# An attention and feed-forward kernel: the order of the work behind the last scores, and three smaller moves of order

## The chip, the cores and the metric

The kernel runs on one core of a Trainium2 chip. The core has five engines that run side by side and meet only through semaphores: TensorE (PE) multiplies matrices, VectorE (DVE) and ScalarE (ACT) work on rows, GpSimd (POOL) does a part of the element-wise work, and SyncE (SP) issues most of the transfers. Each engine executes its own queue in order. Data lies in SBUF (128 partitions); TensorE writes into PSUM, which has eight banks of 512 floats per partition.

The metric is device time in microseconds (us) of one execution, as the median of several. The reader will also meet the span: the time from the first to the last instruction in one profiled execution.

## The reference

A hidden state of 1024 rows by 512 columns goes through attention and then through a feed-forward stage with a router. Both are followed by a layer norm and added to their input:

```
x = x + layernorm(attention(layernorm(x), w_q, w_k, w_v, w_o))
x = x + layernorm(ffn(layernorm(x), base_W, base_b, router_W, router_b, A, B, expert_map))

attention: 32 query heads of 128 columns, 8 key/value heads, causal, softmax(q k / sqrt(128)) v, then w_o
ffn:       base   = x base_W + base_b
           probs  = softmax(x router_W + router_b)        15 columns
           top 8 of probs, mapped to 8 experts -> weight w of each expert
           lora   = (x A * w) B * 2                       8 experts of rank 16
           result = base + lora
```

Everything is in 32-bit floats.

## The kernel before, in words

The 1024 rows are eight row tiles of 128 rows. Attention is cut into 64 blocks: one block is one key/value group g (of eight) and one row tile t. Two neighbouring row tiles of a group are a pair (g, u). The groups 0 to 5 run one after the other; the groups 6 and 7 are interleaved pair by pair, in the order u = 0, 3, 2, 1. So the last blocks are (6,2), (6,3), (7,2), (7,3). The last four row tiles that are completed are named c, d, e, f: tiles 4, 5, 2, 3.

**One block.** `scores` (L601) runs four times per block, once for each 32 rows of the four query heads. It multiplies q and k (tile `s`, in one of two PSUM buffers), adds the mask, takes the negated row maximum `nmax`, computes the exponential with its row sum `total` (tile `p`). Two steps are left to be done inside the next call: `rescale` (L629: the reciprocal `rec` and the multiplication of `p` by it) and `finish` (L634: the transpose of `p` into `T`; after the block's fourth scores, `to_keys` starts 16 transfers that turn `T` into `K`). Two blocks later `weighted_values` multiplies `K` and v (tile `po`, one bank) and copies the result to `attnT`.

**One pair.** Two more blocks on, `project_o_pair` (L711) multiplies a pair's `attnT` with w_o by a scheme with seven half-size products instead of eight. It needs four sums and differences on VectorE first (L720 to L723: `sums` and `attnT`). Its products are `pa` to `pe`; each is merged into `acc`, the running output of the row tiles, by VectorE (L742 for group 0, L744 else). The pieces of the list are, in order, pa (4 pieces), pb (2), pc (2), pd (2), pe (4) and a last step (L751). The last group uses the plain `project_o` (`pO`, merged on L686).

**A completed row tile** then runs through `ffn_norms` (layer norm, adding x, second layer norm to `h`), `ffn_router` (transposes `ptx_h` to `hT`, router products `pl`, exponential, and `route`, eight small VectorE steps from `recr` to `hw`), and `ffn_out` (L840: base products and the transpose `ptw` of `hw`, then `finish` with the last product in `pf`; then y, its statistics, its norm, and the addition to `acc`, L870), and is stored. In `layernorm` (L282) VectorE makes statistics, aggregate and `ve`, GpSimd takes the power -1/2 of one column (`rstd`, L294), and the norm follows on VectorE (L300) or, with a `shift`, on ScalarE (L304).

**PSUM.** Tag `pm` has three banks, which all products other than scores and `po` share. Tag `s` has two buffers, for scores; the base products of some row tiles use these too.

**What sets the order.** A planner orders each engine's instructions by program order and readiness in its own model. An instruction wrapped in `keep` or `order` stays in program order among all instructions so wrapped on its engine; matmuls and transfers always are. The merges, the four sums and many copies are not wrapped in the loop over blocks. In that loop (L1019 to L1074) each block has a list of pieces `then`, of which `run_share` (L962) issues one quarter by cost behind each of the four scores. Small VectorE work waits in the list `deferred`; `work_off` (L587) takes some of it in each `scores`. Behind the loop (L1077 to L1110) the order is written out by hand: `held` takes the place of `deferred`, with one list of steps for each of the rows c, d, e, f, and `go(d, f)` executes the next step of row d and then of row f.

**At the beginning** `input_norms` (L325) normalises the eight input rows: for each row statistics, aggregate, `ve`, the power on GpSimd (`begin`), and then the norm of the row before (`end`).

Of the kernel before, what the change touches and what calls it, by code (L numbers as in the profile page):

```python
# [9 lines left out]
F32 = mybir.dt.float32  # L10
I32 = mybir.dt.int32
AF = mybir.ActivationFunctionType
ALU = mybir.AluOpType
AX = mybir.AxisListType

P = 128
# [6 lines left out]
def kernel(  # L23
# [301 lines left out]
    def input_norms(rows):  # L325

        mvs, rstds = {}, {}

        def begin(t):
            stats = small.tile([P, 6], F32, tag="stats", name=f"stats_x{t}")  # L330
            keep(nc.vector.bn_stats(stats, x_in[:, t, :]))
            mv = mvs[t] = small.tile([P, 2], F32, tag="mv", name=f"mv_x{t}")
            keep(nc.vector.bn_aggr(mv, stats))
            ve = small.tile([P, 1], F32, tag="ve", name=f"ve_x{t}")
            keep(nc.vector.tensor_scalar(ve, mv[:, 1:2], EPS, None, ALU.add))
            rstds[t] = small.tile([P, 1], F32, tag="rstd", name=f"rstd_x{t}")
            keep(nc.gpsimd.tensor_tensor(rstds[t], ve, neg_half, ALU.pow))

        def end(t):
            row = x_in[:, t, :]  # L340
            keep(nc.vector.tensor_scalar(row, row, mvs[t][:, 0:1], rstds[t], ALU.subtract, ALU.mult))

        for n, t in enumerate(rows):
            begin(t)
            if n:
                end(rows[n - 1])
        end(rows[-1])

    def input_turn(t):
# [251 lines left out]
    def scores(g, t, j):  # L601

        n = t * P + (j + 1) * SQ
        full = (t + 1) * P
        name = f"{g}_{t}_{j}"
        s = ps_s.tile([P, S], F32, tag="s", name=f"s_{name}")
        for c0 in range(0, n, QB):
            w = min(QB, n - c0)
            matmul(
                s[:, c0 : c0 + w],  # L610
                qTs[g, t // 2][:, (t % 2) * NSUB + j, :, :].rearrange("p h q -> p (h q)"),
                kTs[g, c0 // QB][:, :w],
                start=True,
                stop=True,
            )
        pin = keep if blocks.index((g, t)) >= N2 + 2 else lambda ins: ins
        rescale_scores()
        keep(nc.vector.tensor_tensor(s[:, n - SQ : n], s[:, n - SQ : n], smask, ALU.add))  # L618
        nmax = small.tile([P, 1], F32, tag="nmax", name=f"nmax_{name}")
        keep(nc.vector.tensor_reduce(nmax, s[:, :n], AX.X, ALU.max, negate=True))  # L620
        p = act.tile([P, S], F32, tag="p", name=f"p_{name}", bufs=3)
        if n < full:
            nc.gpsimd.memset(p[:, n:full], 0.0)  # L623
        total = small.tile([P, 1], F32, tag="total", name=f"total_{name}")
        keep(nc.scalar.activation(p[:, :n], s[:, :n], AF.Exp, bias=nmax, accum_out=total))  # L625
        finish_scores()
        work_off(1 + len(deferred) // 5)

        def rescale():  # L629
            rec = small.tile([P, 1], F32, tag="rec", name=f"rec_{name}")  # L630
            keep(nc.vector.reciprocal(rec, total))  # L631
            keep(nc.scalar.mul(p[:, :n], p[:, :n], rec))  # L632

        def finish():  # L634
            if j == 0:
                turned[g, t] = turn_view(turn_tile("T", g, t), t)
            pin(
                nc.vector.transpose(  # L638
                    turned[g, t][:, :, j, :, :].rearrange("p b k q -> p k b q"),
                    p[:, :full].rearrange("p (k b q) -> p k b q", b=R, q=SQ),  # L640
                )
            )
            if j == NSUB - 1:
                three = (nc.sync, nc.sync, nc.gpsimd)

                at = blocks.index((g, t))
                short = at < 1 or at < N2 and g % 2 and t in (1, 2, 3)
                alone = not short and at < N - 1
                to_keys(g, t, by=three[:1] if alone else three)

        score_tile["rescale"], score_tile["finish"] = rescale, finish
# [59 lines left out]
    def project_o_pair(g, u):  # L711
# [4 lines left out]
        a2 = attnT.pop((g, 2 * u + 1)).rearrange("p (h q) -> p h q", q=P)  # L716
        a11, a12, a21, a22 = a1[:, :hk], a1[:, hk:], a2[:, :hk], a2[:, hk:]
        sums = act.tile([P, 3, hk, P], F32, tag="sums", name=f"sums_{g}_{u}", bufs=1)
        s1, s2, s4 = (sums[:, n] for n in range(3))
        nc.vector.tensor_tensor(s1, a21, a22, ALU.add)  # L720
        nc.vector.tensor_tensor(s2, s1, a11, ALU.subtract)
        nc.vector.tensor_tensor(a21, a11, a21, ALU.subtract)
        nc.vector.tensor_tensor(s4, a12, s2, ALU.subtract)  # L723
        b11, t12, b21, b22 = wo[:, :hk, :hn], wo[:, :hk, hn:], wo[:, hk:, :hn], wo[:, hk:, hn:]
        to = sums_o[u]
        pm = {}
# [113 lines left out]
    def ffn_out(t):  # L840

        pf = []

        def base(k):
            if k == 0:

                if t in (c, e, f):
                    pf.append(ps_s.tile([P, S], F32, tag="s", name=f"pf_{t}")[:, :512])
                else:
                    pf.append(bank(f"pf_{t}"))  # L850
            matmul(pf[0], state["hT", t][:, k, :], weights["base", k], start=(k == 0), stop=False)

        def turn_hw():
            pt = bank(f"ptw_{t}")
            transpose(pt[:, :ER], state.pop(("hw", t)).rearrange("p e r -> p (e r)"), ident)
            hwT = state["hwT", t] = ffn.tile([ER, P], F32, tag="hwT", name=f"hwT_{t}")
            copy = nc.scalar.copy(hwT, pt[:, :P])
            if held:
                keep(copy)

        def finish():
            matmul(pf[0], state.pop(("hwT", t)), bt_sb, start=False, stop=True)
            y = ffn.tile([P, H], F32, tag="hy", name=f"y_{t}", bufs=3)
            order(nc.vector.tensor_tensor(y, pf[0], bias_bc, ALU.add))
            by = nc.vector if t == f else nc.gpsimd
            statistics, norm = layernorm(y, y, f"y{t}", nc.vector if t == f else nc.scalar)

            def add_y():
                norm()
                order(by.tensor_tensor(acc[t], y, acc[t], ALU.add))  # L870
                state["done", t] = True

            defer(t, statistics, add_y)

        w = [(512, lambda k=k: base(k)) for k in range(KC)]
        return w[:2], [(P, turn_hw)], w[2:], [(512, finish)]

    def ffn_store(t):
        assert state["done", t]
# [79 lines left out]
        for _, f in pieces:  # L959
            f()  # L960

    def run_share(pieces, n, m):  # L962

        total = sum(c for c, _ in pieces)
        at = 0
        for c, f in pieces:
            mid = at + c / 2
            if n * total / m <= mid < (n + 1) * total / m:
                f()
            at += c  # L970

# [47 lines left out]
    for i in range(N):  # L1019
# [4 lines left out]
        for t in complete(i, 3):  # L1024
            o = project_o(*blocks[i - 3])
        if i % 2 == 0 and i >= 4 and blocks[i - 4][0] < G - 1:
            o_pair = project_o_pair(*pairs[i // 2 - 2])
        for t in complete(i, 6, 7):
            ends = sum(ffn_out(t), [])
# [9 lines left out]
        if i % 2 and i // 2 + 1 in QW and blocks[i][1] > 1 and i > 3:  # L1039
            cut = len(rest) * 3 // 5  # L1040
            q, rest = weave(q, rest[:cut]), rest[cut:]
        then = begins[:1] + q + ends[:-1] + rest[:4] + ends[-1:] + rest[4:]
        for n in range(NSUB):
            scores(*blocks[i], n)
            run_share(then, n, NSUB)
            m = i // 2 + 1
            if i % 2 == 0 and m in QW:
                if n == 0 and i < N2:
                    combine_x(pairs[m][1], m)
                if n == (1 if i < N2 else 0):  # L1050
                    combine_q(m)
            g, t = blocks[i]
            if g % 2 and g + 1 < G and n == 1:
                if t == 6:
                    combine_k(g + 1)
                if t == 7:
                    combine_v((g + 1) // GV)
            if (i, n) in ((N2, 3), (N2 + 1, 2), (N2 + 2, 2)):
                combine_x(i - N2 + 1, 0)
# [25 lines left out]
        ffn_store(t)  # L1085
    (turn_d, products_d), (turn_e, products_e), (turn_f, products_f) = map(ffn_router, (d, e, f))
    out_c, out_d, out_e, out_f = map(ffn_out, (c, d, e, f))
    run(o_pair[:8] + out_c[0] + out_c[2] + o_pair[8:16] + [turn_d] + o_pair[16:])
    run(attend(N - 2) + [products_d])
    go(d)  # L1090
    run(out_c[1] + project_o(*blocks[N - 2]))
    go(e)
    run(out_c[3])
    go(e, e)
    run(attend(N - 1) + project_o(*blocks[N - 1]))
    go(e, f, c, f, f)
    run(out_d[0] + out_d[1] + out_d[2] + [turn_e] + out_d[3])
    go(f, c)
    run([products_e])
    go(d, e)  # L1100
    run(out_e[0] + out_e[2][:1] + [turn_f] + out_e[2][1:] + [products_f])
    go(d, f)
    run(out_f[0] + out_e[1] + out_f[2][:1] + out_e[3])
    go(e)
    run(out_f[2][1:] + out_f[1])
    go(e)
    run(out_f[3])
    go(f, f)
    for t in (c, d, e, f):
        ffn_store(t)  # L1110

# [40 lines left out]
```

## Time and profile before

| | |
|---|---|
| device time, median of 3 runs | 1064.53 us (1063.63 to 1064.58) |
| device time of the profiled execution | 1063.05 us |
| span of the profiled execution | 1061.3 us |
| mean granted TensorE clock | 0.997 |
| VectorE busy / ScalarE busy | 748.8 us / 478.2 us |
| TensorE busy between 66 and 1000 us | 932.26 of 934.00 us |
| TensorE busy between 1000 and 1052 us | 49.19 of 52.00 us |
| TensorE busy behind 1052 us | 0.15 of 9.30 us |

The span is shorter than the device time by what lies before the first and behind the last instruction. A group in the profile is named by its engine, the line of the program, what it writes and what it reads: "DVE L744 acc<-pa" is VectorE's merge of the product pa. Most matmuls are recorded on L103, which is inside a helper, so the tile's name tells which product it is. A wait is the idle time of an engine ahead of an instruction, with the event that ended it. All times count from the start of the span.

### The profile page before, as it was taken

The page shows a single profiled execution, that of the slowest core. Times are in us where ns is not written, and L with a number is a line of the kernel's source. Part 1 is how long each engine was busy: PE and PEld are TensorE (multiplying, and loading weights), DVE is VectorE, ACT ScalarE, POOL GpSimd, SP SyncE. Part 2 cuts the span into 40 slices and gives each one's busy share as a digit, 9 for nine tenths or more (in the row PEclk, how much of TensorE's full clock was granted, in tenths as well). Part 3 has the DMA queues.
Part 4 walks back from the last instruction along what each step waited for, and adds up shares of the span by engine and source line. Part 5 has one row for each costly group of instructions (what it writes and reads, how often), then busy time and mean ns, then how long its engine had stood idle before and what let it go on. Part 6 is the DMA issues. An engine that isn't in the chain of part 4 may idle for free.

```text
span 1061.3 us, 15618 instructions
## 1 busy us (share of the span) xinstructions
PE 1044.3 (98%) x4854; PEld 730.7 (69%) x4854; DVE 748.8 (71%) x1828; ACT 478.2 (45%) x962; POOL 269.4 (25%) x503
## 2 busy tenths in 40 slices
PE   9999999999999999999999999999999999999996
PEld 7766677767777676767777667767888467466543
DVE  4586657876687766877477776886667966566756
ACT  2655435553344544554244544654334654353421
POOL 2613125241131214241130313442152110111212
PEclk9999999999999999999999999999999999999998
DMA  5146352563125442453324352464333764534331
GB/s 188 33 107 159 72 121 70 152 153 89 24 54 157 102 111 70 117 154 75 70 50 129 100 124 58 131 166 110 87 108 95 169 159 110 146 92 105 80 84 40
DMA packets 78513, 111.99 MB, mean 106 GB/s; under 512 B 18176, under 2 KB 49920, under 8 KB 78432
## 3 DMA queue, kind: packets, MB, share of 16 engines
q1 hardware_dynamic: 74960, 105.71, 39.7%
q0 software_dynamic: 2096, 3.46, 1.4%
q10 hardware_dynamic: 1376, 1.84, 0.5%
q8 instruction: 39, 0.64, 0.3%
q14 instruction: 42, 0.34, 0.1%
HBM read 33.34 MB, written 2.10 MB: 33 GB/s over the span
## 4 chain that ended last, share of the span: by engine, by line
PE 93%; DVE 3%; SPq 1%; ACT 1%; DMA 1%; issue 1%; POOL 0%; POOLq 0%; DVEq 0%; ACTq 0%
PE po L103 23%; PE s L103 21%; PE pq L103 19%; PE pv L103 5%; PE pk L103 5%; PE pe L103 4%; PE pa L103 4%; PE pf L103 3%; PE pO L103 3%; PE pc L103 2%; PE pb L103 2%; PE pd L103 2%; SPq L109 1%; PE pl L103 1%; DVE T L638 1%
## 5 line engine op out<-in xcount | busy, mean ns | idle before, releaser
L632 ACT ACTIVATE p<-p,rec 128x32 f32<-128x32 f32 (+31 forms) x256 | 188.1, 735 | 240.8 <-DVE rec L631 182.2
L103 PE MATMUL po<-K,v 128*128 128x512 f32 x576 | 280.5, 594 | 0.4 <-DMA wo<-in_w_o_dram 0.3
L103 PE MATMUL s<-kT,qT 128*128 128x512 f32 (+15 forms) x768 | 272.4, 464 | 1.3 <-ACT p L625 1.3
L625 ACT ACTIVATE p<-s,nmax 128x32 f32<-128x32 f32 (+31 forms) x256 | 179.3, 700 | 161.3 <-DVE nmax L620 144.8
L638 DVE STREAM_TRANSPOSE T<-p 128x128 f32<-128x128 f32 (+7 forms) x256 | 197.7, 774 | 54.3 <-ACT p L632 42.1
L103 PEld LDWEIGHTS s<-kT,qT 128*128 128x128 f32 x768 | 140.6, 190 | 117.7 <-issue 105.9
L620 DVE TENSOR_REDUCE nmax<-s 128x1 f32<-128x32 f32 (+31 forms) x256 | 180.2, 704 | 7.3
L103 PEld LDWEIGHTS po<-K,v 128*128 128x128 f32 x576 | 103.5, 190 | 59.9 <-issue 50.2
L623 POOL MEMSET p<- 128x96 f32 (+2 forms) x192 | 29.2, 156 | 421.1 <-DVE T L638 387.8
L618 DVE TENSOR_TENSOR s<-s,smask 128x32 f32<-128x32 f32 x256 | 48.0, 187 | 87.8 <-PE s L103 86.9
L103 PE MATMUL pq<-xnT,wq 128*128 128x128 f32 (+1 forms) x608 | 97.5, 308 | 0.0
L103 PEld LDWEIGHTS pq<-xnT,wq 128*128 128x128 f32 x608 | 87.5, 191 | 11.3 <-issue 6.6
L450 DVE TENSOR_TENSOR qT<-pq,qT 128x256 f32<-128x256 f32 x156 | 69.9, 461 | 35.8 <-ACT qT L476 19.8
L188 POOL TENSOR_TENSOR tx<-xnT 128x256 f32<-128x256 f32 x52 | 37.8, 727 | 184.3 <-PE pv L103 95.2
L669 ACT COPY attnT<-po 128x512 f32<-128x512 f32 x64 | 37.3, 583 | 73.1 <-PE po L103 72.8
L103 PE MATMUL pa<-wo,attnT 128*128 128x256 f32 x224 | 58.5, 385 | 0.0
L103 PEld LDWEIGHTS pq<-tx,wq 128*128 128x128 f32 x416 | 53.0, 192 | 7.9 <-issue 7.5
L103 PE MATMUL pq<-tx,sq 128*128 128x128 f32 x416 | 57.5, 275 | 0.0
L103 PEld LDWEIGHTS pq<-tx,sq 128*128 128x128 f32 x416 | 53.4, 192 | 5.7 <-issue 5.0
L103 PE MATMUL pq<-tx,wq 128*128 128x128 f32 x416 | 55.4, 275 | 0.0
L103 PEld LDWEIGHTS pa<-wo,attnT 128*128 128x128 f32 x224 | 41.1, 190 | 14.1 <-issue 9.3
L625 ACT ACTIVATION_READ_ACCUMULATOR p<-s,nmax 128x1 f32 x256 | 49.6, 194 | 0.0
(146 smaller groups left out, 1277.0 us busy)
## 6 DMA issues: line engine op xcount, KB each, us to landing
K<-T SPq DMA_DIRECT2D x128, 128.0 KB, 2.4
K<-T SPq DMA_DIRECT2D x128, 112.0 KB, 2.3
wq<-in_w_q_dram SPq DMA_DIRECT2D x27, 512.0 KB, 5.0
K<-T SPq DMA_DIRECT2D x128, 96.0 KB, 2.2
K<-T SPq DMA_DIRECT2D x128, 80.0 KB, 2.1
wo<-in_w_o_dram SPq DMA_DIRECT2D x32, 256.0 KB, 3.8
K<-T SPq DMA_DIRECT2D x108, 64.0 KB, 2.0
K<-T SPq DMA_DIRECT2D x113, 48.0 KB, 2.0
```

The costliest lines, as they stand in the source:

```text
L103: keep(nc.tensor.matmul(*args, **kw))
L109: keep(by.dma_start(dst, src))
L188: nc.gpsimd.tensor_tensor(dst, p, q, ALU.subtract)
L450: nc.vector.tensor_tensor(dst, src, to, ALU.add)
L618: keep(nc.vector.tensor_tensor(s[:, n - SQ : n], s[:, n - SQ : n], smask, ALU.add))
L620: keep(nc.vector.tensor_reduce(nmax, s[:, :n], AX.X, ALU.max, negate=True))
L623: nc.gpsimd.memset(p[:, n:full], 0.0)
L625: keep(nc.scalar.activation(p[:, :n], s[:, :n], AF.Exp, bias=nmax, accum_out=total))
L632: keep(nc.scalar.mul(p[:, :n], p[:, :n], rec))
L638: nc.vector.transpose(turned[g, t][:, :, j, :, :].rearrange("p b k q -> p k b q"), p[:, :full].rearrange("p (k b q) -> p k b q", b=R, q=SQ),)
L669: copy = nc.scalar.copy(o, po)
```

## The change

Seven places are edited.

- `input_norms`: the statistics of row t stay where they were; aggregate, `ve` and power of row t now stand behind the norm of row t-1.
- `scores`: behind the very last scores of the kernel, `work_off` isn't called. What is deferred there is done later, by the `work_off` behind the loop.
- `project_o_pair`: for the pair (6, 1), whose products run behind the loop, the four sums are kept in program order.
- Block 4: the outstanding `rescale` is issued at the head of the block, ahead of the pair's sums.
- `run_share` takes its limits as fractions. They are the quarters as before, but in blocks with t = 2 of an even group that hold a pair's products the third limit is 0.8 instead of 0.75.
- `ffn_out`: the norm of y is always on ScalarE there, and the addition to `acc` on GpSimd except for row e, whose addition is a step of its own on VectorE. Row f gets a function of its own, `ffn_out_last`: its base product is made as two halves of 256 columns, one in a scores buffer and one in a bank; all of the first half's base pieces come before the second half's; y is added and its statistics are taken half by half, with one step of row e between the halves and one behind the power.
- The order behind the loop: the pair's list is cut at 4 and 10 instead of at 8 and 16, with row c's base products behind pa; row c's `finish` stands behind the last `po` instead of ahead of it; row c's norm and addition stand ahead of row d's `finish`; row f's pieces are interleaved with those of e by halves.

```diff
@@ input_norms
         def begin(t):
             stats = small.tile([P, 6], F32, tag="stats", name=f"stats_x{t}")
             keep(nc.vector.bn_stats(stats, x_in[:, t, :]))
+            return stats
+
+        def power(t, stats):
             mv = mvs[t] = small.tile([P, 2], F32, tag="mv", name=f"mv_x{t}")
...
         for n, t in enumerate(rows):
-            begin(t)
+            stats = begin(t)
             if n:
                 end(rows[n - 1])
+            power(t, stats)
         end(rows[-1])
@@ scores
-        work_off(1 + len(deferred) // 5)
+        if (g, t, j) != (*blocks[-1], NSUB - 1):
+            work_off(1 + len(deferred) // 5)
@@ project_o_pair
+        pin = keep if (g, u) == pairs[-2] else lambda ins: ins
         s1, s2, s4 = (sums[:, n] for n in range(3))
-        nc.vector.tensor_tensor(s1, a21, a22, ALU.add)
+        pin(nc.vector.tensor_tensor(s1, a21, a22, ALU.add))
...
@@ ffn_out
-                if t in (c, e, f):
+                if t in (c, e):
...
-            by = nc.vector if t == f else nc.gpsimd
-            statistics, norm = layernorm(y, y, f"y{t}", nc.vector if t == f else nc.scalar)
-
-            def add_y():
-                norm()
+            statistics, norm = layernorm(y, y, f"y{t}", nc.scalar)
+
+            def add_y(by=nc.gpsimd):
                 order(by.tensor_tensor(acc[t], y, acc[t], ALU.add))
                 state["done", t] = True
-            defer(t, statistics, add_y)
+            if held and t == e:
+                defer(t, statistics, norm, lambda: add_y(nc.vector))
+            else:
+                defer(t, statistics, lambda: (norm(), add_y()))
@@ new
+    def ffn_out_last(t):
+        halves = [slice(n * hn, (n + 1) * hn) for n in range(2)]
+        pf = {}
+
+        def base(n, k):
+            if k == 0 and n == 0:
+                pf[n] = ps_s.tile([P, S], F32, tag="s", name=f"pf_{t}_{n}")[:, :hn]
+            elif k == 0:
+                pf[n] = bank(f"pf_{t}_{n}")[:, :hn]
+            w = weights["base", k][:, halves[n]]
+            matmul(pf[n], state["hT", t][:, k, :], w, start=(k == 0), stop=False)
+
+        def finish(*between):
...
+            for n in range(2):
+                matmul(pf[n], hwT, bt_sb[:, halves[n]], start=False, stop=True)
+                keep(nc.vector.tensor_tensor(y[:, halves[n]], pf[n], bias_bc[:, halves[n]], ALU.add))
+                keep(nc.vector.bn_stats(stats[:, n, :], y[:, halves[n]]))
+                if n == 0:
+                    between[0]()
...
+            keep(nc.gpsimd.tensor_tensor(rstd, ve, neg_half, ALU.pow))
+            between[1]()
+            keep(nc.vector.tensor_scalar(y, y, mv[:, 0:1], rstd, ALU.subtract, ALU.mult))
+            keep(nc.vector.tensor_tensor(acc[t], y, acc[t], ALU.add))
+            state["done", t] = True
+
+        return [[(hn, lambda n=n, k=k: base(n, k)) for k in range(KC)] for n in range(2)], finish
@@ loop over the blocks
         if i % 2 == 0 and i >= 4 and blocks[i - 4][0] < G - 1:
+            if i == 4:
+                rescale_scores()
             o_pair = project_o_pair(*pairs[i // 2 - 2])
...
+        shares = [n / NSUB for n in range(NSUB + 1)]
+        if o_pair and blocks[i][0] % 2 == 0 and blocks[i][1] == 2 and i < N2:
+            shares[3] = 0.8
         for n in range(NSUB):
             scores(*blocks[i], n)
-            run_share(then, n, NSUB)
+            run_share(then, shares[n], shares[n + 1])
@@ behind the loop
-    run(o_pair[:8] + out_c[0] + out_c[2] + o_pair[8:16] + [turn_d] + o_pair[16:])
+    run(o_pair[:4] + out_c[0] + out_c[2] + o_pair[4:10] + [turn_d] + o_pair[10:])
     run(attend(N - 2) + [products_d])
     go(d)
     run(out_c[1] + project_o(*blocks[N - 2]))
     go(e)
-    run(out_c[3])
+    run(attend(N - 1) + out_c[3])
     go(e, e)
-    run(attend(N - 1) + project_o(*blocks[N - 1]))
+    run(project_o(*blocks[N - 1]))
     go(e, f, c, f, f)
-    run(out_d[0] + out_d[1] + out_d[2] + [turn_e] + out_d[3])
-    go(f, c)
+    run(out_d[0] + out_d[1] + out_d[2] + [turn_e])
+    go(c)
+    run(out_d[3])
+    go(f)
     run([products_e])
     go(d, e)
     run(out_e[0] + out_e[2][:1] + [turn_f] + out_e[2][1:] + [products_f])
+    (first, second), finish_f = ffn_out_last(f)
+    run(first + out_e[1])
     go(d, f)
-    run(out_f[0] + out_e[1] + out_f[2][:1] + out_e[3])
+    run(second[:1] + out_e[3])
     go(e)
-    run(out_f[2][1:] + out_f[1])
-    go(e)
-    run(out_f[3])
-    go(f, f)
+    run(second[1:2] + out_f[1] + second[2:])
+    finish_f(lambda: go(e), lambda: go(e))
```

More of the change, by code (lines that the diff above doesn't have):

```diff
@@ L718, in project_o_pair @@
         sums = act.tile([P, 3, hk, P], F32, tag="sums", name=f"sums_{g}_{u}", bufs=1)
+        pin = keep if (g, u) == pairs[-2] else lambda ins: ins
         s1, s2, s4 = (sums[:, n] for n in range(3))
-        nc.vector.tensor_tensor(s1, a21, a22, ALU.add)
-        nc.vector.tensor_tensor(s2, s1, a11, ALU.subtract)
-        nc.vector.tensor_tensor(a21, a11, a21, ALU.subtract)
-        nc.vector.tensor_tensor(s4, a12, s2, ALU.subtract)
+        pin(nc.vector.tensor_tensor(s1, a21, a22, ALU.add))
+        pin(nc.vector.tensor_tensor(s2, s1, a11, ALU.subtract))
+        pin(nc.vector.tensor_tensor(a21, a11, a21, ALU.subtract))
+        pin(nc.vector.tensor_tensor(s4, a12, s2, ALU.subtract))
         b11, t12, b21, b22 = wo[:, :hk, :hn], wo[:, :hk, hn:], wo[:, hk:, :hn], wo[:, hk:, hn:]
@@ L875, in ffn_out @@
         w = [(512, lambda k=k: base(k)) for k in range(KC)]
         return w[:2], [(P, turn_hw)], w[2:], [(512, finish)]
+    def ffn_out_last(t):
[9 more added lines that the diff above has]
+        def finish(*between):
+            hwT = state.pop(("hwT", t))
+            y = ffn.tile([P, H], F32, tag="hy", name=f"y_{t}", bufs=3)
+            stats = small.tile([P, 2, 6], F32, tag="stats2", name=f"stats_y{t}", bufs=1)
+            for n in range(2):
[4 more added lines that the diff above has]
+                    between[0]()
+            mv = small.tile([P, 2], F32, tag="mv", name=f"mv_y{t}")
+            keep(nc.vector.bn_aggr(mv, stats))
+            ve = small.tile([P, 1], F32, tag="ve", name=f"ve_y{t}")
+            keep(nc.vector.tensor_scalar(ve, mv[:, 1:2], EPS, None, ALU.add))
+            rstd = small.tile([P, 1], F32, tag="rstd", name=f"rstd_y{t}")
+            keep(nc.gpsimd.tensor_tensor(rstd, ve, neg_half, ALU.pow))
[4 more added lines that the diff above has]
+        return [[(hn, lambda n=n, k=k: base(n, k)) for k in range(KC)] for n in range(2)], finish
@@ L960, in run, with run_share @@
             f()
-    def run_share(pieces, n, m):
+    def run_share(pieces, a, b):
         total = sum(c for c, _ in pieces)
@@ L967, in run_share @@
             mid = at + c / 2
-            if n * total / m <= mid < (n + 1) * total / m:
+            if a * total <= mid < b * total:
                 f()
```

## The prediction

> **What bounds the kernel.** I read the busy line first, then TensorE's own waits, then the timeline around each wait, and the chain of waits for what follows TensorE's last matmul.
>
> ```profile
> PE 1044.3 (98%) x4854; PEld 730.7 (69%) x4854; DVE 748.8 (71%) x1828; ACT 478.2 (45%) x962; POOL 269.4 (25%) x503
> ```
>
> TensorE is busy 98% of the span, so only two things can move the time: a moment in which it has nothing to do, and the tail behind its last matmul, which ends at 1052.15 of 1061.3. This is nearly all the waiting (us in total, times, longest):
>
> ```profile
> PE s L103 <- ACT p L625: 1.3, 4, 0.3
> PE pb L103 <- DVE top L817: 1.2, 1, 1.2
> PE pc L103 <- DVE rec L631: 0.9, 1, 0.9
> PE pc L103 <- DVE acc L744: 0.5, 1, 0.5
> PE pO L103 <- ACT attnT L669: 0.7, 1, 0.7
> PE pf L103 <- ACT hwT L857: 0.4, 1, 0.4
> PE ptx_x L106 <- DVE K_x L341: 0.4, 1, 0.4
> ```
>
> The timeline places them: the four s at 289.88, 413.00, 535.27 and 658.09 (one in each of the groups 2 to 5, before the last scores of its third block), one pc at 64.26 (block 4), everything else but the first ptx_x behind the last scores. Of those, pO:
>
> ```profile
> 1030.87 0.59 ACT L669 COPY attnT<-po 128x512 f32<-128x512 f32 x1 [6.88 <-PE po L103]
> 1031.51 3.70 PE L103 MATMUL pO<-wo,attnT 128*128 128x512 f32 x8 [0.68 <-ACT attnT L669]
> ```
>
> From start to start these waits are larger than listed, since the modelled end of a matmul runs on by some 0.15.
>
> The timeline of the end, of VectorE and GpSimd:
>
> ```profile
> 1047.73 1.27 POOL L870 TENSOR_TENSOR acc<-y,acc 128x512 f32<-128x512 f32 x1 [2.85 <-ACT y L304]
> ...
> 1047.93 1.10 DVE L821 TENSOR_TENSOR sel<-pr,rest 128x15 f32<-128x15 f32 x1
> ...
> 1053.65 1.26 POOL L870 TENSOR_TENSOR acc<-y,acc 128x512 f32<-128x512 f32 x1 [1.23 <-ACT y L304]
> ...
> 1054.24 0.15 DVE L292 TENSOR_SCALAR ve_y<-mv_y 128x1 f32<-128x1 f32 x1
> 1054.87 0.55 POOL L294 TENSOR_TENSOR rstd_y<-ve_y,neg_half 128x1 f32<-128x1 f32 x1
> 1055.45 0.55 DVE L300 TENSOR_SCALAR y<-y,mv_y,rstd_y 128x512 f32<-128x512 f32 x1 [1.05 <-POOL rstd_y L294]
> 1056.03 0.69 DVE L870 TENSOR_TENSOR acc<-y,acc 128x512 f32<-128x512 f32 x1
> ```
>
> To see: a 15-column sel takes 1.10 (0.17 elsewhere) and ends as GpSimd's add ends, and the last power waits behind another of those adds. From the last add's end, 1056.72, to the end of the span is 4.58, the store, which stays.
>
> **Part by part.**
>
> **Input rows** (L325). norm(t-1) now comes before aggr and ve of row t. Row 0's norm waits for its power (ends 6.47) and not for ve at 6.62: it ends some 0.2 earlier, but the copy behind the transposes waits for ScalarE's table load until 7.85 and starts at 7.97 today: worth **0.1**. Rows 1 to 3 then take 1.66 each and not 1.47, because power, norm, aggr and ve follow one another; row 2's norm ends about 10.3, its transposes start about 10.75. Covered.
>
> **Block 4.** The rescaling's reciprocal moves from 61.82 to about 60.0, where VectorE is idle until 60.35, and ScalarE's multiply from 62.07 to 60.4. pc waits for the bank of pa, whose copy (L742) starts at 63.46, behind the sums, the mask, the max and the transpose. None of them waited for the multiply, so only the reciprocal's 0.07 to 0.15 leaves the queue: **0.1**. Upper end 1.1, the whole gap, if the planner then puts the copy before the transpose; lower end 0.
>
> **Third blocks of even groups.** The condition holds in blocks 18 and 34 only (groups 2 and 4; group 0 has no o_pair there). The list has 14 pieces of 256 columns, one of 512 and one of 1: 4097. Cut at 0.75 the first pe piece (middle at 3200) is in the last share, at 0.80 (3278) it is in the third; the next (3456) isn't. So one piece of 0.43 goes before s. s is ready at about 289.87 and PE stands from 289.44: the 0.44 is filled. The next scores then start at 291.92; they need the buffer whose exponential ends at 291.68, so 0.24 remains. Two blocks: **0.85**; 0 if that margin is used up.
>
> **Behind the last scores.** Today pa ends at 1007.17 + 8 x 0.215 = 1008.89, pb starts at 1010.31, ends at 1011.17, pc starts at 1011.88: 2.1 lost, because the route of row c alternates with the four sums on VectorE. Then pf of c (3.44) follows, of which pc and pd have the cover. The change puts pf of c directly behind pa, so pb is due at 1012.33. VectorE: last transpose but one to 1009.24, then the reciprocal, which must wait for ScalarE's accumulator at 1009.73, four sums (0.35 each) to 1011.35, the last transpose to 1012.05, then the route, 2.1 when undisturbed. pb's sum is ready at 1010.7: no wait. But pb, pc, pd now stand in a row on three banks, of which pl of c holds one until the route is done. pa's merge (0.65) fits at 1009.24 or 1012.25, so pc goes on time at 1013.19; pd, due at 1014.05, waits for pb's merge (0.95, from 1013.4) or for the route: 0.3 to 0.6, and pe, due some 1.3 later, may wait 0 to 0.4 more. I take 0.6: **2.1 + 0.1 - 0.6 = 1.6**. The last transpose ends 3.4 earlier (1015.48 today), so its 11 transfers on SP and 5 on GpSimd start at about 1012.4 (SP is then through with the block before) and land by 1022; its matmuls are due at 1025. The rows reloaded behind them on SP come earlier too.
>
> **The last po.** Its two out_c[3] matmuls (0.86) go between po and pO, whose wait is 0.83 from po's end to pO's start: **0.8**. y of row c is added 4 us later and stands before norm(e) on VectorE; everything of e up to its rstd is still done before pO ends, as it must be.
>
> **The last rows.** Work on TensorE is the same. Take pl of f, which ends at 1045.84, as zero in both. Today: route f ends at +4.15, 0.93 of it sel under GpSimd's add; y of f is added at +6.74, after VectorE waited 0.73 for row e's rstd; last add ends at +10.88. After: the copy of hwT of e now precedes row d's norm on ScalarE, so GpSimd's add of d starts at about +3.2, when the route ends (+3.2). y of e at +3.4, its ve to +5.2, its power +5.9. TensorE's two half products end at +5.05 and +5.5. VectorE: half add 0.42 (row of 256 columns, 0.42 to 0.46), half statistics (no row; between 0.34 and 0.68 of the full one, taken 0.40), shift of e, half add, half statistics, aggr, ve: to +7.45. Then the power beside e's add (0.69, now VectorE's), norm 0.55, add 0.69: **+9.4 when nothing collides, 1.45 saved.**
>
> Here a rule speaks against the change. Row first: powers beside a VectorE norm took 0.71 to 0.79 instead of 0.55 (at 6.85, 15.73 and 1038.55). The Trainium skill, "SBUF — State Buffer", section "Who interferes with whom", says that a VectorE instruction with two SBUF inputs shuts out a GpSimd one that reads SBUF for its whole length if it started first. Row e's add starts some 0.15 before the last power. By the rule the power waits the rest of 0.69 and the saving is 1.0; by the row it loses 0.2 and the saving is 1.25. I take **1.2**. The sel above agrees with the rule; an add from PSUM at 1019.04 beside GpSimd's add took its plain 0.69, so row y of e isn't held up.
>
> Earlier, go(c) before out_d[3] moves row c's GpSimd add from 1043.11 to about 1041.9 on today's clock, off the route of e (pr there 0.86 for 0.23). It can hold the norm of h_f, whose transposes have 1.5 spare. Worth nothing.
>
> **Sum.** 0.1 + 0.1 + 0.85 + 1.6 + 0.8 + 1.2 = 4.65, say 4.7. The profiled execution took 1063.05, 1.75 outside its span of 1061.3; the change would make it 1058.35. That execution lies 1.48 below the median shown, 1064.53, so the forecast is **1059.8**.
>
> **Rivals.** What can be told from no change is 0.2%, 2.1 us.
> *VectorE becomes the bound in the pair's products.* The planner puts every merge behind the transpose, the route and the shift: pa's merge ends at 1015.0, pc starts 1.9 late. For it: the merges aren't pinned, the sums now are. Against: today they were set between the route's steps. The 1.6 falls to 0.4: 1061.0.
> *It doesn't do what it says.* The share edit only moves its wait to the next scores (margin 0.24), the end stays behind e's chain, the banks eat the rest; only the 0.8 and the two 0.1 hold with some of the end, 1.5 in all: 1063.0. Against: each of these would have to fail.
> *Slower: the planner's order in the loop.* Merges, sums of the pairs and copies of 60 blocks aren't pinned, and their order hangs on what stands before. If a score wait of 0.44 appears in every second block, 29 of them, 12.8 is lost: 1059.8 + 12.8 = 1072.6; slower from 16 places on (7.0). For it: the same 0.33 stands in four groups, so one order repeats. Against: between 66 and 1000 PE is busy 932.3 of 934.0 and VectorE 72%.
>
> **Numbers.** Forecast 0.58 (own range 1058.3 to 1061.2), first rival 0.18, second 0.12, slower one 0.12. Faster 0.76, within 0.2% 0.12, slower 0.12. Range 1057.6 (block 4's whole gap and no bank wait) to 1063.6.
>
> **What would show it.** Right: no s wait at the third block of groups 2 and 4, still one in 3 and 5; pb without a wait; a small wait at pd; no pO wait; sel under 0.3; last add some 9.5 to 9.8 after pl of f. Wrong: a pc wait above 1 behind the last scores, new s waits in the loop, or a power above 0.9 at the end.

## The result, and the profile after

The changed kernel takes 1059.37 us (median of 6 runs, 1058.72 to 1060.68) against 1064.32 us before (6 runs). The ratio is 0.9955, 95% interval 0.9942 to 0.9968, that is 3.4 to 6.2 us less. The profiled execution took 1059.33 us; its span is 1057.34 us, 3.92 less than the 1061.26 before.

TensorE's own waits after the change (us in total, times, longest us):

```profile
PE idle L106 <- POOL ident masks.py:199: 1.5, 1, 1.5
PE ptx_x L106 <- DVE K_x L344: 0.7, 1, 0.7
PE s L103 <- ACT p L629: 0.7, 2, 0.3
PE pc L103 <- DVE acc L748: 0.7, 1, 0.7
PE po L103 <- DMA wo<-in_w_o_dram: 0.6, 1, 0.6
PE pv L103 <- ACT xnT L321: 0.6, 2, 0.3
PE pd L103 <- DVE hw L836: 0.3, 1, 0.3
```

Gone are pb, the second pc and pO behind the last scores, pf at the very end, and two of the four s. New is pd. The pc in the list is that of block 4, which waited 0.9 before the change. The two s that stay are at 412.65 and 657.14, in groups 3 and 5, which the change leaves alone. The first transposes (ptx_x) and one po (for w_o) wait 0.3 longer than in the profile before.

Because TensorE does the same work in every kernel, the time can be cut at fixed instructions. This table goes from start to start, except where an end is named. The marks are the last pa (that of the pair behind the last scores), the transpose of row c's hw (it follows pl of d), the last pO, pl of row f and the end of the last addition to acc.

| stretch, us | before | after | gained |
|---|---|---|---|
| start to last pa | 1007.17 | 1006.09 | 1.08 |
| last pa to transpose of hw | 15.67 | 14.51 | 1.16 |
| to last pO | 8.67 | 7.83 | 0.84 |
| to pl of f | 13.35 | 13.34 | 0.01 |
| to the end of the last addition | 11.86 | 11.03 | 0.83 |
| to the end of the span | 4.54 | 4.54 | 0.00 |

Between the last pa and the end of the span 2.84 are gained. The 1.08 ahead of it hold 0.86 of the third blocks and 0.29 of block 4; the rest, a loss of 0.07, is a sum of small differences, which go both ways in the runs below.

The timeline around the new wait (VectorE, weight loads and matmuls):

```profile
1013.09 0.29 DVE L836 TENSOR_TENSOR hw<-pl,w 128x128 f32<-128x128 f32 x1
...
1013.43 1.13 PE L103 MATMUL pd<-wo,sums 128*128 128x256 f32 x4 [0.29 <-DVE hw L836]
...
1014.42 0.42 PEld L106 LDWEIGHTS ptx_h<-ident,h 128*128 128x128 f32 x4 [0.26 <-DVE acc L750]
...
1015.21 0.73 PEld L103 LDWEIGHTS pe<-wo,sums 128*128 128x128 f32 x4 [0.38 <-DVE acc L750]
```

pc started at 1012.11 and needs 0.86, so pd was due at 1012.97. It started 0.46 later, when hw had read the router products and their bank was free. The transposes then waited for the merge of pb and pe for that of pc; by the po behind pe (1017.04) the stretch has lost 1.05.

The end, VectorE and GpSimd:

```profile
1050.33 0.15 DVE L913 TENSOR_SCALAR ve_y<-mv_y 128x1 f32<-128x1 f32 x1
1050.40 0.68 DVE L874 TENSOR_TENSOR acc<-y,acc 128x512 f32<-128x512 f32 x1
1050.62 0.86 POOL L915 TENSOR_TENSOR rstd_y<-ve_y,neg_half 128x1 f32<-128x1 f32 x1 [1.69 <-DVE ve_y L913]
1051.52 0.55 DVE L917 TENSOR_SCALAR y<-y,mv_y,rstd_y 128x512 f32<-128x512 f32 x1 [0.44 <-POOL rstd_y L915]
1052.11 0.69 DVE L918 TENSOR_TENSOR acc<-y,acc 128x512 f32<-128x512 f32 x1
```

The power takes 0.86 for one column, 0.31 more than alone, and ends 0.40 behind row e's addition.

What stands behind the last addition is not only the store. Each engine runs a DRAIN at the end of the program. These are those of GpSimd and of SyncE, which waits for the stores (shortest, middle and longest in ns, first and last start in us):

```profile
L1201 POOLq DRAIN  x3: 46/102/5961, 1050.6 to 1057.1; - x3
L1201 SPq DRAIN  x3: 7/7/7, 1055.3 to 1056.8; - x3
```

The last store has landed at 1054.83, and SyncE comes to its DRAIN at 1055.34. GpSimd's long one lasts from 1050.60 to 1056.56: it ends 5.07 behind the end of GpSimd's last piece of work, the power (1051.49), and 0.78 before the end of the span. Before the change it is the same: the power ends at 1055.41, the DRAIN at 1060.49, and SyncE comes to its own at 1059.27. So the span ends 5.85 behind the last power, in both kernels.

### The profile page after: what moved, and what is told of

Same layout as the page of the kernel before. It is cut to its first block, busy times and chain, and to the rows that moved or that the text cites. A ratio compares the mean times of both kernels' runs of the same rounds, so it can differ in the third digit from the quotient of the medians.

```text
span 1057.3 us, 15637 instructions
## 1 busy us (share of the span) xinstructions
PE 1043.3 (99%) x4864; PEld 732.0 (69%) x4864; DVE 748.2 (71%) x1831; ACT 477.9 (45%) x962; POOL 267.5 (25%) x502
## 4 chain that ended last, share of the span: by engine, by line
PE 92%; DVE 3%; SPq 2%; ACT 1%; DMA 1%; issue 1%; POOL 0%; POOLq 0%; ACTq 0%; DVEq 0%
PE po L103 22%; PE s L103 21%; PE pq L103 19%; PE pv L103 5%; PE pe L103 4%; PE pk L103 4%; PE pa L103 4%; PE pf L103 3%; PE pO L103 3%; PE pc L103 2%; PE pb L103 2%; PE pd L103 2%; SPq L109 2%; PE pl L103 1%; DVE nmax L624 1%
## 5 line engine op out<-in xcount | busy, mean ns | idle before, releaser
L636 DVE RECIPROCAL rec<-total 128x1 f32<-128x1 f32 x256 | 39.2, 153 | 15.7 <-ACT p L629 14.5
```

## The experiments

The theory under test: the time is TensorE's waits, place by place, plus the chain behind the last matmul; each part of the change gives what its own stretch shows. The rivals are written in the expectations. All ratios are to the kernel before on the same chip. Executions with the same instructions ahead of the last pa reached it up to 1.8 us apart, so the verdicts rest on the stretches, which agree to 0.04 wherever their instructions are the same. Each stretch is read from one profiled execution of its kernel.

**The pair's part undone.**

```diff
-    run(o_pair[:4] + out_c[0] + out_c[2] + o_pair[4:10] + [turn_d] + o_pair[10:])
+    run(o_pair[:8] + out_c[0] + out_c[2] + o_pair[8:16] + [turn_d] + o_pair[16:])
...
-        if (g, t, j) != (*blocks[-1], NSUB - 1):
-            work_off(1 + len(deferred) // 5)
+        work_off(1 + len(deferred) // 5)
...
-        pin = keep if (g, u) == pairs[-2] else lambda ins: ins
+        pin = lambda ins: ins
```

> The changed kernel with the pair's part undone: list cut at 8 and 16 again, the deferred work taken in the last scores, sums not kept in order. If the gain there is TensorE's filled wait (span of the changed kernel 1057.3, its milestones show 1.2 gained between pa and the po behind the pair), the waits of pb (1.2) and pc (0.5) come back, the waits of pd and pe (1.0 from start to start) go, and the span is 1.2 longer: 1058.5, time some 1060.5. If the end of the kernel hangs on VectorE's chain of the last rows and not on when TensorE gets there, the span stays within 0.3 of 1057.3.

Measured: 1061.48 us, ratio 0.9972 (0.9959 to 0.9984), span 1059.4. Its timeline has both waits back:

```profile
1010.13 1.10 PE L103 MATMUL pb<-wot,sums 128*128 128x256 f32 x4 [1.27 <-DVE top L822]
1011.70 1.10 PE L103 MATMUL pc<-wot,attnT 128*128 128x256 f32 x4 [0.47 <-DVE acc L749]
```

The stretch from the last pa to the transpose of hw is 15.69, and everything behind it is as in the changed kernel (7.83, 13.33, 11.03). So the 1.16 belongs to this part, and it arrives at the end undiminished. The span grew by 2.1 and not by 1.2, because this execution reached the last pa 0.88 later.

**Only the order on VectorE undone**, the new cut of the list kept (the last two edits of the diff above).

> The changed kernel with the new cut of the pair's list, but the deferred work taken in the last scores and the sums free again, as before the change. If the cover by row c's base products is what counts, pb still finds its sum ready, the route ends earlier than in the changed kernel (no sum is kept ahead of it) and pd waits less: the stretch from the last pa to the transpose of row c's hw is 14.5 or up to 0.4 shorter. If the order on VectorE is what counts, pb or pc waits again and the stretch is over 15.

Measured: 1058.92 us, ratio 0.9958 (0.9945 to 0.9972), stretch 14.19. pb and pc start on time. The route alternates with the sums again and hw ends at 1012.00, ahead of pd (1013.47, no wait); only the transposes and pe wait. The gain comes from the cover alone; keeping the sums ahead of the deferred route costs 0.32 here.

**Row c's finish back ahead of the last po.**

```diff
-    run(attend(N - 1) + out_c[3])
+    run(out_c[3])
     go(e, e)
-    run(project_o(*blocks[N - 1]))
+    run(attend(N - 1) + project_o(*blocks[N - 1]))
```

> The changed kernel with row c's finish ahead of the last po again. If that move alone fills the wait for the copy of attnT, pO waits 0.7 again and the span is 0.8 longer: 1058.1, time some 1060.2. If another part of the change had already taken the wait away (K arrives 3 us earlier, the copy finds ScalarE free), pO waits less than 0.2 and the span stays.

Measured: 1060.62 us, ratio 0.9962 (0.9947 to 0.9976), span 1058.6. Among TensorE's waits:

```profile
PE pO L103 <- ACT attnT L674: 0.7, 1, 0.7
```

The stretch from the transpose of hw to the last pO is 8.68 instead of 7.83, the others are unchanged. So this move alone fills the wait, and no other part of the change had taken it away.

**The third limit back at 0.75** (`shares[3] = 0.75`).

> The changed kernel with the third limit at 0.75. If the piece that moved is what fills the wait, s waits 0.33 again in the third blocks of groups 2 and 4, so four times in all, and everything behind is 0.86 later: span 1058.2, time some 1060.2. If the moved limit only shifts the wait to later scores, less than 0.3 is lost.

Measured: 1060.69 us, ratio 0.9962 (0.9947 to 0.9977), span 1059.3. TensorE's waits for scores:

```profile
PE s L103 <- ACT p L629: 1.3, 4, 0.3
```

Four again, at 290.81, 413.97, 536.25 and 659.17. From the second to the fourth scores of the third blocks of groups 2 and 4 it takes 5.28 each, as before the change, and 4.85 each in the changed kernel: 0.86 for both. In the changed kernel s, pe and the next scores pass without any wait (289.68, 290.43, 291.73), so nothing was moved to later scores. The time is 1.3 longer and not 0.86; the profiled execution lost 1.1 more than that ahead of the last pa.

**Input rows and block 4 as before.**

```diff
             stats = begin(t)
+            power(t, stats)
             if n:
                 end(rows[n - 1])
-            power(t, stats)
...
-            if i == 4:
-                rescale_scores()
```

> The changed kernel with the input rows and block 4 as they were. If these two gave what the trace shows, the stretch from the first pa to the first pc of block 4 is 6.6 again instead of 6.3, and TensorE's first product starts about 0.1 later: 0.4 on a span of 1057.3, less than runs differ by in the first 60 us. If block 4 gained only the reciprocal's slot, the stretch is 6.4.

Measured: 1059.42 us, ratio 0.9959 (0.9945 to 0.9972), span 1057.5. First pa to first pc of block 4 takes 6.58; it is 6.59 before the change and 6.30 or 6.31 in every kernel with the edit. How this comes about is seen in the changed kernel's VectorE:

```profile
61.91 0.19 DVE L622 TENSOR_TENSOR s<-s,smask 128x32 f32<-128x32 f32 x1
62.01 0.70 DVE L643 STREAM_TRANSPOSE T<-p 128x512 f32<-128x512 f32 x1
62.63 0.69 DVE L624 TENSOR_REDUCE nmax<-s 128x1 f32<-128x544 f32 x1
63.24 0.67 DVE L748 COPY acc<-pa 128x512 f32<-128x512 f32 x1
```

With the multiply done early the planner puts the transpose between the mask and the maximum that reads it, and mask to copy takes 1.33 instead of 1.57. For the input rows nothing can be said: with them undone the first transposes start at 7.06, with them at 7.14, and in other runs of the edited order between 6.91 and 7.25 where they waited at all.

That the 0.29 reaches the end isn't shown: the time with both edits undone is that of the changed kernel (1059.42 against 1059.37), and executions differ by more than 0.29. Just ahead of block 4, near 57, the scores wait 0.3 to 0.7 for qT in ten of the twelve profiled executions with the two edits (0.33 in the second execution of the changed kernel below), in none of the two without. Two are too few to say that the edits bring this wait.

**Row d's norm and addition ahead of row f's first half.**

```diff
-    run(first + out_e[1])
     go(d, f)
+    run(first + out_e[1])
```

> The changed kernel with row d's shift, norm and addition ahead of row f's first half again, so that GpSimd's addition runs beside row f's route. If the lock on the shared port is what made sel slow, GpSimd's addition starts some 1.3 earlier, sel takes about 1.0 instead of 0.17, hw of f ends near 5.2 behind pl of f instead of 3.2 plus, the transpose of hw waits some 0.4, and row f's last addition ends 0.5 to 0.6 later: span 1057.9. If the slow sel was chance, it takes 0.2 and the span stays at 1057.3 within 0.2.

Measured: 1060.23 us, ratio 0.9957 (0.9942 to 0.9972), last stretch 11.38 instead of 11.03:

```profile
1045.88 1.26 POOL L874 TENSOR_TENSOR acc<-y,acc 128x512 f32<-128x512 f32 x1 [3.75 <-ACT y L304]
1045.89 0.16 DVE L825 MATCH_REPLACE8 rest<-top,pr 128x15 f32<-128x15 f32 x1
1046.08 1.09 DVE L827 TENSOR_TENSOR sel<-pr,rest 128x15 f32<-128x15 f32 x1
```

sel is held until GpSimd's addition has ended; all eight sel of the changed kernel take 0.17. Of sel's 0.92 only 0.35 reaches the end, less than the 0.5 to 0.6 expected, because row e's y has to wait for its product anyway. The rest of the last rows' 0.83 isn't divided further: no run takes back the halves of row f.

**Row e's addition behind row f's** (`between[1]()` moved two lines down).

> The changed kernel with row e's addition behind row f's, so that nothing on VectorE with two inputs from SBUF runs beside the last power. If the shared port holds the power back, it takes 0.55 instead of 0.86 and row f's addition ends 0.3 earlier, 10.7 behind the start of pl of f instead of 11.0; row e's addition then ends 0.4 later than the last addition does today, and with it the span grows by some 0.4. If the power is long for another reason (a late start of GpSimd), it stays at 0.86.

Measured: 1059.38 us, ratio 0.9958 (0.9943 to 0.9973), span 1058.8, of which 1.6 is lost ahead of the last pa.

```profile
1052.24 0.55 POOL L915 TENSOR_TENSOR rstd_y<-ve_y,neg_half 128x1 f32<-128x1 f32 x1 [1.69 <-DVE ve_y L913]
1052.83 0.55 DVE L916 TENSOR_SCALAR y<-y,mv_y,rstd_y 128x512 f32<-128x512 f32 x1 [0.73 <-POOL rstd_y L915]
```

The power starts 0.29 behind the start of ve, as in the changed kernel, and takes 0.55. So it is VectorE's addition that holds it back, by 0.31. Row f's addition ends 10.72 behind pl of f, row e's 11.32; from pl of f to the end of the span it is 15.39, against 15.57 in the changed kernel. The expected loss of 0.4 didn't come, because it was counted from the last addition. GpSimd's DRAIN ends 5.07 behind the power here too, at 1057.87, so that it comes 0.31 earlier with the power. Now SyncE's wait for row e's late store lasts longer than that, to 1057.94, and takes back a part.

**A cover for the bank waits: the po of the last block but one between pc and pd.**

```diff
-    run(o_pair[:4] + out_c[0] + out_c[2] + o_pair[4:10] + [turn_d] + o_pair[10:])
-    run(attend(N - 2) + [products_d])
+    run(o_pair[:4] + out_c[0] + out_c[2] + o_pair[4:8] + attend(N - 2))
+    run(o_pair[8:10] + [turn_d] + o_pair[10:] + [products_d])
```

> The changed kernel with the po of the last block but one (2.6 of TensorE's work that needs no bank of the three) set between pc and pd. If pd, the transposes and pe wait for banks that VectorE frees too late (1.05 from start to start between pc and the po), these waits go and the stretch from the last pa to the transpose of row c's hw falls from 14.5 to 13.5 to 13.8; K of that block, due to land near 1013, may make the po wait up to 0.3. If the loss there is TensorE's own (short transposes, loads of weights), the stretch stays at 14.5 within 0.2.

Measured: 1058.49 us, ratio 0.9952 (0.9938 to 0.9965), span 1056.6, stretch 13.47 instead of 14.51.

```profile
1013.26 2.74 PE L103 MATMUL po<-K,v 128*128 128x512 f32 x6
1013.36 0.29 DVE L836 TENSOR_TENSOR hw<-pl,w 128x128 f32<-128x128 f32 x1
...
1015.83 1.03 PE L103 MATMUL pd<-wo,sums 128*128 128x256 f32 x4
...
1016.69 0.60 PE L106 MATMUL ptx_h<-ident,h 128*128 128x128 f32 x4
...
1017.13 1.03 PE L103 MATMUL pe<-wo,sums 128*128 128x256 f32 x4
```

No wait is left: K was there in time, hw ends behind the po's start and is covered. 1.04 of the 1.05 come back, so the banks and VectorE's pace were the loss.

**Cover and a shorter end together.**

```diff
             mv = small.tile([P, 2], F32, tag="mv", name=f"mv_y{t}")
             keep(nc.vector.bn_aggr(mv, stats))
+            low = small.tile([P, 1], F32, tag="shift", name=f"low_y{t}")
+            keep(nc.vector.tensor_scalar(low, mv[:, 0:1], -1.0, None, ALU.mult))
+            keep(nc.scalar.activation(y, y, AF.Identity, bias=low))
...
-            keep(nc.vector.tensor_scalar(y, y, mv[:, 0:1], rstd, ALU.subtract, ALU.mult))
-            keep(nc.vector.tensor_tensor(acc[t], y, acc[t], ALU.add))
+            keep(nc.vector.scalar_tensor_tensor(acc[t], y, rstd, acc[t], ALU.mult, ALU.add))
```

> The po set between pc and pd as above, and the end of row f shortened: y less its mean on ScalarE beside the power, then one VectorE instruction that multiplies by rstd and adds to acc, in place of a norm and an addition. If both causes are as told, the stretch behind the last pa falls by 0.7 to 1.0 and the end from pl of f to the last addition from 11.0 to 10.5: span 1.2 to 1.5 below the changed kernel's, time some 1058.0. If ScalarE's step ends later than the power, the second part gives less than 0.2.

Measured: 1058.81 us, ratio 0.9952 (0.9939 to 0.9964), span 1056.2. From pl of f to the last addition it is 10.56 instead of 11.03, as forecast, but the time isn't lower than with the cover alone: from the last addition to the end of the span it is now 5.07 instead of 4.54.

```profile
1049.44 0.86 POOL L918 TENSOR_TENSOR rstd_y<-ve_y,neg_half 128x1 f32<-128x1 f32 x1 [1.75 <-DVE ve_y L916]
1050.33 0.75 DVE L920 SCALAR_TENSOR_TENSOR acc<-y,rstd_y,acc 128x512 f32<-128x512 f32 x1 [0.44 <-POOL rstd_y L918]
```

The power ends at 1050.30, GpSimd's DRAIN at 1055.37, 5.07 later, and the span at 1056.15. The shorter end lies behind the power, so it can't move the end of the span; the power itself even ends 0.05 later behind pl of f (9.77 for 9.72), because one more small step stands ahead of it.

**The three on one chip**, the changed kernel and the two versions.

> The changed kernel itself, on the same chip as the next two. Time 1059.4, last pa to transpose of hw 14.5, pl of f to last addition 11.0.

> The po set between pc and pd, on the same chip. If the 1.04 that the stretch lost is real for the whole kernel, its median is about 1.0 below that of the changed kernel beside it; if the end takes it back, the medians are within 0.4.

> As the one before, and row f's end shortened by 0.47. If that reaches the end of the execution, its median is 1.5 below the changed kernel's; if the 5.1 from the last addition to the end, 0.6 longer than elsewhere, is no chance, it is 1.0 below, as with the cover alone.

Measured: 1059.65 us (1059.13 to 1059.96) for the changed kernel, 1058.69 us (1058.27 to 1059.16) with the cover, 1058.72 us (1058.16 to 1059.62) with both. The stretches repeat: 14.52, 13.47, 13.47; ends 11.03, 11.03, 10.56. The cover gives 0.96 by the medians. The intervals of the ratios to before, 0.9965 (0.9951 to 0.9978) and 0.9956 (0.9944 to 0.9969), overlap, so that the cover is faster as a whole rests on the stretch and on five runs each. The shorter end is taken back a second time (5.07 from the last addition to the end, 4.55 in the changed kernel), and again the DRAIN ends 5.07 behind the power. In all fourteen profiled executions it does so, within 0.01, and in all but that with row e's addition last the span ends 5.85 or 5.86 behind the power. What the DRAIN does in that time is open.

## Why the prediction was right

The time, 1059.37 for 1059.8, the sign and the mechanism were right: the gain is TensorE's waits that were filled, and the end behind the last matmul. That the time came so close is in part luck, as the sum behind the table shows. By its terms:

| term | forecast | measured |
|---|---|---|
| input rows | 0.1 | not resolved |
| block 4 | 0.1 (0 to 1.1) | 0.29 |
| third blocks | 0.85 | 0.86 |
| pair behind the last scores | 1.6 | 1.16 |
| last po | 0.8 | 0.84 |
| last rows | 1.2 | 0.83 |

The single stretches sum to 3.98 where 4.55 was forecast for these five: the terms were 0.57 too high. The medians differ by 4.95, the spans of the two profiled executions by 3.92. The 0.97 between the medians and the stretches isn't explained by any instruction. It lies within the interval. The profiled execution before lies 1.27 below the median of its kernel and the one after 0.04 below, and where the other executions before lose this time no trace shows.

- **Third blocks, last po.** Right to 0.04, and each shown by its undoing. The next scores didn't wait, so the margin of 0.24 sufficed.
- **Pair.** The mechanism was right, that pb, pc, pd in a row on three banks cost something at pd and pe. The mis-sized term is the 0.6 of bank waits: it is 1.05, and 2.1 + 0.1 - 1.05 gives the 1.16 to 0.01. pd alone lost 0.46, within the 0.3 to 0.6 written down; but the prediction gave pe 0 to 0.4 and the transposes nothing, and took 0.6 in all, where all three waited one after another. The merge of pa was placed between the sums, and the route was not interrupted by merges.
- **Last rows.** Two terms are off. Row e's y was forecast at 3.4 behind pl of f's end and came at 3.67: the copy of hwT of e on ScalarE ended at 1045.21, so its product waited for it, which the sum had left out. And the power lost 0.31 rather than the 0.25 by which the 1.2 is below the undisturbed 1.45. Together these are 0.33 of the 0.37 missing. The last addition came 10.05 behind the end of pl of f, later than the 9.5 to 9.8 named as a sign.
- **The end.** The prediction read the 4.58 behind the last addition as the store, which stays. It stays, but as GpSimd's DRAIN: the end hangs on the last power, 1.31 ahead of the end of the last addition in both kernels. So the 0.83 is the same counted to either, and the reading did no harm here; it failed in the expectation for the shorter end.
- **Rule against row.** The row of the trace gave a loss of 0.2, the rule that the prediction cites about 0.45. With 0.31 the rule's direction holds (the addition started first, and without an addition beside it the power takes 0.55), its full length doesn't: the power ended 0.40, not 0.55, behind the addition.
- **Input rows.** Rows 1 to 3 were to take 1.66 each. Their norms start 1.67, 1.49 and 1.48 apart: the power, no longer beside a norm, takes 0.55 instead of 0.78.
- **Block 4.** It was said that only the reciprocal's slot leaves the queue, since nothing waited for the multiply. What happened in its place is that the transpose, ready earlier, was put ahead of the maximum: 0.07 come from the slot and 0.24 from the stretch between mask and copy, and 0.02 are lost behind it. The trace before leaves it open whether the transpose did wait: it starts at 62.83, 0.04 behind the end of the multiply.
- **Collisions.** sel is under 0.3 as foretold; the earlier addition of row c (1038.68) touched no route, and the norm h of row f kept its 0.55.
- **The rivals.** Every merge behind the route: partly so, since pb's and pc's merges did stand behind it, but pa's didn't and pc wasn't late. That the change does little: the share edit's wait moved to no later scores, and the end moved with the power. Score waits in every second block: none in the profile after; the one near 57 in other executions is a single one of 0.7 at most, not 29.

## What to carry to other kernels

Where one engine is busy nearly all the time, list its waits with their places, and count what work that needs nothing from the late engine can be put into each. Here the waits filled behind the last scores were gained in full at the end. Products that share few buffers need other work between them while the merges catch up: the same cover, set after the first product, left 1.05 open, which a second piece of cover removed. Small steps that end a chain are worth checking against what runs beside them, since the power of one column took half as much again beside VectorE's addition. And find out what the end of the execution hangs on before shortening the last chain: here it was GpSimd's last instruction, and a shorter chain behind it gave nothing.

## What was not expected of the hardware

GpSimd's DRAIN at the end of the program ended 5.07 behind GpSimd's last instruction in all fourteen profiled executions, and in thirteen of them it was the last thing that the end waited for.

Kernels with the same instructions ahead of the last pa reached it between 1005.88 and 1007.71. Part of this are two waits for transfers, at 151 (from none to 1.26, for K) and at 327 (0.22 to 0.74, for w_o or K), and the scores' wait near 57 (none to 0.7), which come and go from run to run. Each can be as large as what a single part of the change moves.

Of VectorE's steps that lay beside an addition of GpSimd, sel (two inputs in SBUF) and the 15-column pr (0.86, before the change) were held to its end; a match-replace that started 0.01 behind it was not (0.16), nor a statistics step at 1039.11 in the changed kernel (0.68).
